# A two-layer decoder on one Trainium2 core: six of eight lanes send each token to its two experts in 128-row tiles, two lanes keep all eight experts

## Chip, core and metric

The kernel runs on one core of one Trainium2 chip. The metric is device time in microseconds (us), the median of three runs of one execution each. The engines are called as in the profile: PE (TensorE matmul), PEld (TensorE's weight load), DVE (VectorE), ACT (ScalarE), POOL (GpSimd), SP (SyncE, here only a queue that issues DMAs).

## What is computed

A decoder of two layers on x of shape (16, 128, 256), all in float32. Six blocks are added to x one after the other, each on a layer-normed x:

```python
x = x + L0_attn(ln(x))             # one causal head
x = x + L0_xattn(ln(x), ctx)       # 16 heads over a context
x = x + L0_ffn(ln(x))              # 16 blocks of 64, 4 chosen per token
x = x + L1_attn(ln(x))             # 16 heads
x = x + L1_xattn(ln(x), ctx, cell) # 16 heads, windows of 64, rotary, masked by cell
x = x + L1_ffn(ln(x))              # the experts: the block that is changed
```

The last block, with 8 experts of width 128, two of them for each token, and a shared expert of width 256 for all tokens:

```python
scores = sigmoid(x @ gate_weight.T)                    # (2048, 8)
topk_w, topk_idx = top_k(scores, 2)
topk_w = 2.5 * topk_w / (topk_w.sum(-1) + 1e-20)
h = silu(x @ w_gate[e].T) * (x @ w_up[e].T)            # for each expert e
routed = sum over the two chosen e of topk_w[e] * (h @ w_down[e].T)
out = routed + shared_swiglu(x)
```

## The kernel before

The 16 sequences are worked in 8 lanes of two sequences, 256 tokens each. A lane is a chain of Python generators: `layer_0(l)`, then `layer_1(l)` (self attention and windowed attention), then `expert_ffn(l)`. Each generator yields the engine that it wants next and the buffers it takes. The class `Turns` is a planner: it keeps an estimate of when each engine is free and when each buffer comes back, picks the thread that can go on first, and records its instructions. So the order of instructions on every engine is fixed when the program is built, by the planner's estimates; on the chip each engine works through its own list in order and waits on semaphores. All matmuls are recorded on the helper's line 126, transposes on L131, DVE work on L135, ACT on L139, POOL on L145, so the profile tells them apart by tile names.

`more()` starts lanes: at most `IN_FLIGHT = 5` at once, all eight `layer_0` first, then the eight `layer_1`, then `expert_ffn` as lanes end. The weights of the routed experts (`gu`, two tiles of 128x2048, and `down`, 128x2048) take the SBUF place of layer 0's weights, so `late_weights()` loads them after the last lane's layer 0.

`expert_ffn(l)` runs every token of a lane through all eight experts. Normalised x is transposed (`tps`), the router's scores (`rt`) are ranked, and a table of shares, zero for experts not chosen, is turned with PE (`ptt`). For each of 8 + 2 halves (8 routed experts and the shared expert's two halves) PE computes gate and up with 4 matmuls of 128x128 weights over 256 tokens (`gu`), ACT and DVE make the gated product (`sg`, `hm`), and for the routed ones PE spreads the shares over the rows (`wb`) and DVE multiplies. At the end 20 matmuls (`y1`, in the profile `y<-down,hm` and `y<-L_shared,hm`) sum all experts for both sequences, DVE adds that to x and SP stores the lane.

```python
for f in range(NE + DC):                 # one(f): 8 routed experts, 2 shared halves
    for n in range(2):                   # gate, up
        for d in range(DC):              # 256 inputs in two chunks
            q.matmul(gu[:, n, :], wt, xT[:, d, :], start=d == 0, stop=d == DC - 1)
```

A float32 matmul counts as two PE instructions in the profile, a transpose as one. Buffers are counted by `LIMITS`: 4 PSUM banks, 2 score buffers `s` (two banks each), 6 `xn`, 5 `xT`, 4 `v`, and so on. SBUF is nearly full.

Of the kernel before, what the change touches and what calls it, by code (L numbers as in the profile page):

```python
# [9 lines left out]
F32 = mybir.dt.float32  # L10
I32 = mybir.dt.int32
BF16 = mybir.dt.bfloat16
# [18 lines left out]
BPC = P // 64  # L31
NE, TOPE = 8, 2


OUT = -(2.0**100)
EPS = 1e-05
# [4 lines left out]
C_ONES = C_HEADS + HR  # L41
C_TRI16 = C_ONES + HC
C_TRI8 = C_TRI16 + NB * NB
C_ALL = C_TRI8 + NE * NE


COLS = [
# [23 lines left out]
PE, DVE, ACT, POOL, SP = "PE", "DVE", "ACT", "POOL", "SP"  # L71

WHOLE, BY_ROWS, BY_COLUMNS, BY_BOTH = range(4)


class Turns:
# [70 lines left out]
    def moved(self, n_bytes):  # L147

        self.moves = max(self.moves, self.now.at) + n_bytes / 300.0
        self.now.at = self.moves + 2000.0  # L150

    def fetch(self, out, src):

# [57 lines left out]
    def run(self, more):  # L211

        while True:
            more()
            best = None
            for i, th in enumerate(self.threads):
                if th.ask is None:
                    continue
                engine, takes = th.ask
                at = self.reach(th, engine)  # L220
                ok = True
                for tag, n in takes.items():
                    left = sorted(self.tiles[tag])
                    if not n:
                        continue
                    if len(left) < n:
                        ok = False
                        break
                    at = max(at, left[n - 1])
                if ok and (best is None or (at, th.rank, i) < best[0]):  # L230
                    best = (at, th.rank, i), th
            if best is None:
                assert not self.threads, "no thread can go on"
                return
            (at, _, _), th = best
            engine, takes = th.ask
            for tag, n in takes.items():
                self.tiles[tag].sort()
                del self.tiles[tag][:n]
            th.at, th.last = max(th.at, at), engine  # L240
            self.resume(th, None)


class Thread:
    def __init__(self, gen, rank, at, parent):
        self.gen, self.rank, self.at, self.parent = gen, rank, at, parent
        self.last, self.ask, self.waits, self.children, self.result = None, None, 0, [], None


@with_exitstack  # L250
def decoder(ctx: ExitStack, tc: tile.TileContext, a: dict, out: bass.AP):
# [4 lines left out]
    work = ctx.enter_context(tc.tile_pool(name="work", bufs=2))  # L256
    small = ctx.enter_context(tc.tile_pool(name="small", bufs=4))
    ps_s = ctx.enter_context(tc.tile_pool(name="ps_s", bufs=2, space=PSUM))
    ps = ctx.enter_context(tc.tile_pool(name="ps", bufs=4, space=PSUM))

    dram = ctx.enter_context(tc.tile_pool(name="dram", bufs=1, space=bass.MemoryType.DRAM))

    def bank(shape, name):
        return ps.tile(shape, F32, tag="bank", name=name)
# [40 lines left out]
    def along(t, n):  # L305
# [8 lines left out]

    experts = keep.tile([P, NE, P], BF16, name="experts")

    scaled_bias = {
        name: keep.tile([P, DC], F32, name=f"scaled_{name}") for name in ("L0_xattn_bq", "L1_attn_b_q", "L1_xattn_b_q")
    }
# [2 lines left out]
    for t in chosen:  # L322
        nc.gpsimd.memset(t, 0.0)

    v_tiles = [keep.tile([P, G, H * HA + CT - HA], F32, name=f"v{i}") for i in range(4)]
    for t in v_tiles:
        nc.gpsimd.memset(t, 1.0)

# [1 line left out]
    for t in tops:  # L330
        nc.gpsimd.memset(t, 0.0)


    LIMITS = dict(
        bank=4, s=2, oT=1, xn=6, xT=5, qk=5, qs=3, kb=3, v=4, p=4, oS=2, on=4, hm=8, tmp=3, rank=2, selT=2, p0=2,
        pT0=2, unseen=4, chosen=3, swap=2, words=1, top=3,
    )
    q = Turns(nc, LIMITS)

# [146 lines left out]
    def attention(qT, kb, v, j, unseen=None, to=None):  # L486
# [5 lines left out]

        js = slice(j * S, (j + 1) * S)
        yield PE, dict(s=2)
        ss = banks()
        for e in range(DC):
            for r in range(4):
# [9 lines left out]
        for t2, s in enumerate(ss):  # L507
            q.dve(
                "tensor_reduce", top[:, t2 * 2 * RT : (t2 + 1) * 2 * RT].rearrange("p (h d) -> p h d", d=HD)[:, :, 0:DC],
                s.rearrange("p r h e s -> p (r h) e s"), AX.X, ALU.max, negate=True,  # L510
            )
            q.give("s")
        yield PE, dict(bank=1)
        t = bank([P, S], "topT")
        q.transpose(t, top, ident)
# [12 lines left out]
        )  # L528
        q.give("tmp")
        yield PE, dict(s=2)  # L530
        ss = banks()
        for e in range(DC):
            for h in range(HR):
# [10 lines left out]
        def exponentials(s):  # L544
            yield ACT, dict(p=1)
            p = new("p", [P, HC, S], "p")
            q.act("activation", p, s.rearrange("p r h e s -> p (r h e) s"), AF.Exp)
            q.give("s")
            return p

        pTs = yield [exponentials(s) for s in ss]
        yield PE, dict(oT=1, bank=1)

        oT = bank([P, H // 4, S], "oT")
# [14 lines left out]
        q.act("copy", oS, oT)  # L569
        q.give("oT")  # L570
        q.give("bank")
        yield PE, dict(bank=1)
        o = bank([P, H // 4, S], "o")
        for t4 in range(H // 4):
# [327 lines left out]
        ]  # L902
        q.give("xn")

    def gated(sg, gu, h, half=0.5):

        yield DVE
        q.dve("scalar_tensor_tensor", sg, sg, 1.0, gu[:, 0, :], ALU.add, ALU.mult)
        q.dve("scalar_tensor_tensor", h, sg, half, gu[:, 1, :], ALU.mult, ALU.mult)
        q.give("tmp")  # L910
        q.give("bank")

# [51 lines left out]
    def expert_ffn(l):  # L964
# [31 lines left out]
        def one(f):  # L996
            yield PE, dict(bank=1, tmp=1)
            gu = bank([P, 2, GT], "gu")
            for n in range(2):
                for d in range(DC):  # L1000
                    if f < NE:
                        wt = w["gu"][d][:, f * D + n * P : f * D + (n + 1) * P]
                    else:
                        wt = w["shared"][:, d, n * D + (f - NE) * P : n * D + (f - NE + 1) * P]
                    q.matmul(gu[:, n, :], wt, xT[:, d, :], start=d == 0, stop=d == DC - 1)
            yield ACT
            h = hm[f // 2][:, f % 2, :]
            sg = new("tmp", [P, GT], "sg")
            q.act("activation", sg, gu[:, 0, :], AF.Tanh, scale=0.5)
            yield from gated(sg, gu, h)  # L1010
            if f < NE:
                yield PE, dict(bank=1)
                wb = bank([P, GT], "wb")
                q.matmul(wb, experts[:, f, :], wT, start=True, stop=True)
                yield DVE
                q.dve("tensor_tensor", h, wb, h, ALU.mult)
                q.give("bank")
# [15 lines left out]
            q.dve("tensor_tensor", x[l][:, j, :], x[l][:, j, :], y, ALU.add)  # L1033
            q.give("bank")
        nc.sync.dma_start(out[l * G : (l + 1) * G].rearrange("b s d -> s b d"), x[l])
        experts_ended[0] += 1


    arrives = {}
# [35 lines left out]
    def tables():  # L1075
        yield DVE
        q.dve("tensor_copy", ident16, ident)
        for name, scale in (("L0_xattn_bq", 0.25), ("L1_attn_b_q", 0.0625), ("L1_xattn_b_q", 0.25)):
            q.dve("tensor_scalar", scaled_bias[name], cols[:, slice(*COL_AT[name])], scale, None, ALU.mult)
        yield DVE  # L1080
        q.dve("memset", blocks, 0.0)
        q.dve("tensor_copy", blocks[0:NB], along(ident[0:NB, 0:NB], P // BPC))
        yield DVE
        parts = small.tile([P, NE], F32, tag="parts", name="parts", bufs=1)
        q.dve("tensor_tensor", parts, ident[:, 0:NE], ident[:, NE : 2 * NE], ALU.add)
        q.dve("tensor_tensor", parts, parts, ident[:, 2 * NE : 3 * NE], ALU.add)
        q.dve("tensor_copy", experts, along(parts, P))


    experts_ended = [0]  # L1090
    begun, ended = [0], []
    blocks_left = [NL]
    experts_begun = [0]
# [13 lines left out]
    def layer_0(l):  # L1107
        yield from causal_attention(l)
        yield from context_attention(l)
        yield from block_ffn(l)  # L1110
        blocks_left[0] -= 1
        if blocks_left[0] == 0:
            late_weights()
        ended.append(l)

    def layer_1(l):
        yield from self_attention(l)
        yield from windowed_attention(l)
        ended.append(l)

    IN_FLIGHT = 5

    def more():
        n = begun[0]
        if n < IN_FLIGHT and n not in arrives:
            return
        if n < 2 * NL and n - len(ended) < IN_FLIGHT and (n < NL or n - NL in ended[:NL]):
            begun[0] += 1
            q.start((layer_0 if n < NL else layer_1)(n % NL), n, q.free_at[PE] if n >= IN_FLIGHT else arrives[n])
            return  # L1130
        if ready and experts_begun[0] < min(len(ended) - NL, experts_ended[0] + 3):
            l = ended[NL + experts_begun[0]]
            experts_begun[0] += 1
            q.start(expert_ffn(l), 2 * NL + l, max(q.free_at[PE] - 5000, ready[0]))

    with tc.manual_schedule(engines={mybir.EngineType.PE, mybir.EngineType.DVE, mybir.EngineType.Activation, mybir.EngineType.Pool, mybir.EngineType.SP}):
        q.start(first_loads(), 0)
        q.start(tables(), 0, 16000.0)
        q.start(later_loads(), 3 * NL, 60000.0)
        q.start(hidden_by_mask(), 0, 8000.0)  # L1140
        q.start(hidden_by_window(), 3 * NL, 100000.0)
        q.run(more)

def _constants():
# [18 lines left out]
    t[:, C_HEADS : C_HEADS + HR] = np.arange(P)[:, None] // HD % HR == np.arange(HR)[None, :]  # L1165
    for n, at in ((NB, C_TRI16), (NE, C_TRI8)):
        t[:, at : at + n * n] = np.tril(np.ones((n, n)), -1).reshape(1, n * n)
    return t


# [66 lines left out]
```

## Time and profile before

| what | value |
|---|---|
| median of three runs (lowest, highest) | 850.72 us (850.51, 851.03) |
| profiled execution, its own time | 849.42 us |
| its span, first to last instruction | 847.4 us |
| PE busy | 818.3 us, 97% of the span |
| PEld, DVE, ACT, POOL busy | 661.2, 481.7, 372.1, 350.0 us |
| DMA queue of SP, share of 16 engines | 13.8% |
| TensorE clock granted, mean | 0.998 |

The page has the busy time of each engine, the span cut in 40 slices, the chain of work that ended last, and groups of instructions by tile. A group's busy time counts overlaps with the next group twice, since matmuls are pipelined; start to start distances in the timeline give the pitch at which a stream of them really runs. A "busy" PE is not waiting for another engine; whether it could do the same with fewer matmuls is not seen in that number.

### The profile page before, as it was taken

The page shows a single profiled execution, that of the slowest core. Times are in us where ns is not written, and L with a number is a line of the kernel's source. Part 1 is how long each engine was busy: PE and PEld are TensorE (multiplying, and loading weights), DVE is VectorE, ACT ScalarE, POOL GpSimd, SP SyncE. Part 2 cuts the span into 40 slices and gives each one's busy share as a digit, 9 for nine tenths or more (in the row PEclk, how much of TensorE's full clock was granted, in tenths as well). Part 3 has the DMA queues.
Part 4 walks back from the last instruction along what each step waited for, and adds up shares of the span by engine and source line. Part 5 has one row for each costly group of instructions (what it writes and reads, how often), then busy time and mean ns, then how long its engine had stood idle before and what let it go on. Part 6 is the DMA issues. An engine that isn't in the chain of part 4 may idle for free.

```text
span 847.4 us, 19890 instructions
## 1 busy us (share of the span) xinstructions
PE 818.3 (97%) x8128; PEld 661.2 (78%) x8128; DVE 481.7 (57%) x1218; ACT 372.1 (44%) x801; POOL 350.0 (41%) x606
## 2 busy tenths in 40 slices
PE   6999999999999999999979999999999999999998
PEld 5877678778787777876758867878778888888887
DVE  5446565565262644546685686675566575555533
ACT  4555434362544354626747565565343424212111
POOL 5345454153165443636777875445422331100000
PEclk9999999999999999999999999999999999999999
DMA  8325202112100000160120102010100100000000
GB/s 285 113 72 162 70 25 34 36 38 78 40 1 13 2 2 2 39 187 1 52 64 13 53 3 74 3 48 30 51 2 1 63 13 2 13 1 14 13 12 13
DMA packets 41178, 36.83 MB, mean 43 GB/s; under 512 B 6784, under 2 KB 36608, under 8 KB 40448
## 3 DMA queue, kind: packets, MB, share of 16 engines
q1 hardware_dynamic: 41088, 35.57, 13.8%
q8 instruction: 64, 1.05, 0.5%
q14 instruction: 26, 0.21, 0.1%
HBM read 27.16 MB, written 4.19 MB: 37 GB/s over the span
## 4 chain that ended last, share of the span: by engine, by line
PE 85%; DVE 6%; POOL 4%; ACT 2%; issue 2%; DMA 1%; SPq 0%; POOLq 0%; ACTq 0%; DVEq 0%
PE gu L126 16%; PE s L126 14%; PE y L126 14%; PE pj L126 11%; PE pr L126 9%; PE hp L126 7%; PE oT L126 5%; PE tps L131 3%; PE o L131 2%; PE rt L126 2%; DVE top L135 1%; POOL rstd L145 1%; DMA swap<-kT 1%; ACT p L139 1%; PE wb L126 1%
## 5 line engine op out<-in xcount | busy, mean ns | idle before, releaser
L135 DVE TENSOR_REDUCE top<-s 128x8 f32<-128x1024 f32 x96 | 112.8, 1217 | 31.1 <-PE s L126 31.0
L139 ACT ACTIVATE p<-s 128x1024 f32<-128x1024 f32 x96 | 94.6, 1027 | 60.0 <-PE s L126 60.0
L126 PE MATMUL gu<-srcT,gu 128*128 128x256 f32 x512 | 118.4, 380 | 1.5 <-DVE hm L135 0.9
L145 POOL TENSOR_TENSOR qs<-qT,less 128x512 f32<-128x512 f32 x48 | 61.0, 1272 | 112.1 <-ACT less L139 105.7
L126 PEld LDWEIGHTS gu<-srcT,gu 128*128 128x128 f32 x512 | 93.8, 190 | 16.8 <-DVE hm L135 1.2
L139 ACT ACTIVATE sg<-gu 128x256 f32<-128x256 f32 x80 | 30.8, 385 | 116.6 <-PE gu L126 111.2
L145 POOL TENSOR_SCALAR rstd<-mv 128x2 f32<-128x2 f32 x72 | 16.6, 230 | 121.0 <-DVE mv L135 116.6
L126 PE MATMUL hp<-srcT,L_w 128*128 128x256 f32 x256 | 65.9, 387 | 0.0
L126 PE MATMUL s<-qs,kb 32*128 32x128 f32 x1536 | 59.4, 286 | 5.7 <-POOL qs L145 2.9
L126 PEld LDWEIGHTS s<-qs,kb 32*128 32x128 f32 x1536 | 49.5, 188 | 16.9 <-issue 7.3
L126 PE MATMUL y<-L_w,hm 128*128 128x256 f32 x256 | 59.0, 383 | 0.0
L126 PE MATMUL y<-down,hm 128*128 128x256 f32 x256 | 58.4, 381 | 0.0
L145 POOL TENSOR_SCALAR kb<-kT,consts 128x256 f32<-128x256 f32 x96 | 53.1, 566 | 10.3 <-ACT kT L139 9.7
L126 PE MATMUL s<-kb,qT 32*128 32x256 f32 x768 | 56.5, 401 | 0.6 <-DVE top L135 0.6
L126 PE MATMUL oT<-p,v 128*32 128x128 f32 x1536 | 52.5, 276 | 2.1 <-ACT p L139 2.0
L135 DVE TENSOR_TENSOR x<-x,y 128x256 f32<-128x256 f32 x32 | 13.4, 418 | 71.4 <-PE y L126 71.4
L126 PEld LDWEIGHTS y<-L_w,hm 128*128 128x128 f32 x256 | 47.7, 190 | 8.0 <-issue 1.5
L145 POOL TENSOR_TENSOR rstd<-rstd,power 128x2 f32<-128x2 f32 x72 | 51.3, 713 | 6.0
L126 PEld LDWEIGHTS hp<-srcT,L_w 128*128 128x128 f32 x256 | 44.3, 190 | 11.5 <-issue 3.3
L126 PEld LDWEIGHTS y<-down,hm 128*128 128x128 f32 x256 | 47.8, 190 | 6.3 <-issue 0.2
L145 POOL TENSOR_TENSOR eq<-eq,consts 128x512 bf16<-128x512 bf16 (+1 forms) x16 | 15.0, 940 | 89.7 <-DVE eq L135 89.6
L135 DVE SCALAR_TENSOR_TENSOR sg<-sg,gu 128x256 f32<-128x256 f32 x80 | 33.2, 415 | 31.3 <-ACT sg L139 31.1
(149 smaller groups left out, 1625.1 us busy)
## 6 DMA issues: line engine op xcount, KB each, us to landing
unseen<-hidden SPq DMA_DIRECT2D x128, 64.0 KB, 2.4
c<-in_ctx SPq DMA_DIRECT2D x16, 256.0 KB, 3.0
x<-in_x SPq DMA_DIRECT2D x8, 256.0 KB, 6.3
L_w<-in_L_w SPq DMA_DIRECT2D x2, 1024.0 KB, 6.4
hidden<-plain SPq DMA_DIRECT2D x32, 64.0 KB, 1.5
gu<-in_L_gu SPq DMA_DIRECT2D x2, 1024.0 KB, 5.2
swap<-kT SPq DMA_DIRECT2D x16, 128.0 KB, 2.1
swap<-qT SPq DMA_DIRECT2D x16, 128.0 KB, 2.1
```

The source lines that it names most:

```text
L126: self.nc.tensor.matmul(out, lhsT, rhs, **kw)
L131: self.nc.tensor.transpose(out, src, ident)
L135: getattr(self.nc.vector, name)(out, *args, **kw)
L139: getattr(self.nc.scalar, name)(out, *args, **kw)
L145: getattr(self.nc.gpsimd, name)(out, *args, **kw)
```

## The change

Lanes 0 to 2 and lanes 3 to 5 become two groups with `GROUPS = ((0,1,2),(3,4,5))`; lanes 6 and 7 keep the eight experts for every token as before.

- `routing(l)`, at the end of `layer_1(l)` of a grouped lane: scores and ranks as before, then for each token and choice its row in a list sorted by expert (counts by five small bf16 matmuls `n`, with running totals kept in SBUF), then four indirect DMAs from POOL that scatter the normalised rows to DRAM (`to_experts`). The shared expert stays dense (`shared`).
- `plan(g)`, when a group's three lanes are routed: some 22 small DVE operations that work out for each of 19 tiles of 128 rows its expert and its rows (`tile_expert`, `tile_rows`). 19 is 2 x 768 / 128 + 7, so that each expert's last tile may be partly empty whatever the routing.
- `expert_tile(g, i)`, 19 for each group: POOL gathers 128 rows by an indirect DMA, PE transposes them (`xgt`), loads the expert's number into a PE register (`value`), and multiplies with weights whose address comes from that register: two matmuls of 256 columns for gate and up (`gu2`), a transpose (`hT2`), one for down (`y2`). ACT copies `xgT`, `hT`, `yo` and issues the DMA that stores the result in DRAM (`by_experts`).
- `combining(g, l)`, when all 19 tiles are done: four gathers by POOL for each lane, each followed by one DVE multiply-add into x; then SP stores the lane.
- `blank(g)` writes zeros over `to_experts` from SP early on.
- Lanes start in another order (`TURN`): `layer_0` of lanes 0 to 5, then `layer_1` of a lane and `layer_0` of a later one in turns. A tie in the planner goes to threads that hold the score buffers. Fewer buffers: `xn` 5 for 6, `xT` 4 for 5, `v` 3 for 4, `hm` 7 for 8, `swap` 1 for 2; 6 `xe` are new; `p0` and `pT0` 3 for 2.

```diff
+GROUPS = ((0,1,2),(3,4,5))
+    def value(self, src, most):
+        self.charge(PE, 300.0)
+        return self.nc.values_load(
+            src, engines=(mybir.EngineType.PE,), min_val=0, max_val=most,
...
+    def indexed(self, out, out_index, src, src_index):
+        at = lambda i: None if i is None else bass.IndirectOffsetOnAxis(ap=i, axis=0)
...
+        self.nc.gpsimd.indirect_dma_start(out, at(out_index), src, at(src_index))
-                if ok and (best is None or (at, th.rank, i) < best[0]):
+                key = (at, not (th.holds or "s" in takes), th.rank, i)
-        bank=4, s=2, oT=1, xn=6, xT=5, qk=5, qs=3, kb=3, v=4, p=4, oS=2, on=4, hm=8, tmp=3, rank=2, selT=2, p0=2,
-        pT0=2, unseen=4, chosen=3, swap=2, words=1, top=3,
+        bank=4, s=2, oT=1, xn=5, xT=4, qk=5, qs=3, kb=3, v=3, p=4, oS=2, on=4, xe=6, hm=7, tmp=3, rank=2, selT=2, p0=3,
+        pT0=3, unseen=4, chosen=3, swap=1, words=1, top=3,
+    def routing(l):
...
+            for j in range(G):
+                q.matmul(n[:, j, :], before, sel[:, j, :], start=True, stop=j == 0)
+                for i in range(j):
+                    q.matmul(n[:, j, :], ones, sel[:, i, :], start=False, stop=i == j - 1)
...
+            for j in range(G):
+                for k in range(TOPE):
+                    yield POOL
+                    i = j * TOPE + k
+                    q.indexed(g.to_experts, to[:, i : i + 1], xn[:, j, :], None)
...
+        yield [choice(), shared(l, xT)]
+    def expert_tile(g, i):
+        yield POOL, dict(xe=2)
+        xg = new("xe", [P, D], "xg")
+        q.indexed(xg, None, g.to_experts, g.tile_rows[:, i : i + 1])
+        yield PE, dict(bank=1)
+        t = bank([P, DC, S], "xgt")
+        for d in range(DC):
+            q.transpose(t[:, d, :], xg[:, d * P : (d + 1) * P], ident)
...
+        q.act("copy", xgT, t)
+        yield PE, dict(bank=1, tmp=1)
+        gu = bank([P, 2, P], "gu2")
+        at = q.value(g.tile_expert[0:1, i : i + 1], (NE - 1) * D)
+        for d in range(DC):
+            q.matmul(gu, xgT[:, d, :], w["gu"][d][:, bass.ds(at, D)], start=d == 0, stop=d == DC - 1)
...
+        q.act("activation", sg, gu[:, 0, :], AF.Tanh, scale=0.5)
+        q.dve("scalar_tensor_tensor", sg, sg, 1.0, gu[:, 0, :], ALU.add, ALU.mult)
+        q.dve("scalar_tensor_tensor", h, sg, 0.5, gu[:, 1, :], ALU.mult, ALU.mult)
...
+        q.transpose(t, h, ident)
+        q.act("copy", hT, t)
+        q.matmul(y, hT, w["down"][:, bass.ds(at, D)], start=True, stop=True)
+        q.act("copy", yo, y)
+        q.load(g.by_experts[i * P : (i + 1) * P, :], yo, engine=ACT)
...
+    def combining(g, l):
...
+            q.indexed(y, None, g.by_experts, by[:, j * TOPE + k : j * TOPE + k + 1])
+            q.dve("scalar_tensor_tensor", x[l][:, j, :], y, weight[l][:, j, k : k + 1], x[l][:, j, :], ALU.mult, ALU.add)
...
+    def blank(g):
...
+        for e in range(NE):
+            q.load(some, zero.to_broadcast(list(some.shape)))
+            q.now.at += 10000.0
+    def sorted_experts(g):
+        yield from plan(g)
+        yield [expert_tile(g, i) for i in range(g.tiles)]
+        yield [combining(g, l) for l in g.lanes]
+    TURN = [(0, l) for l in range(6)]
+    for l in range(NL):
+        TURN += [(1, l), (0, l + 6)] if l + 6 < NL else [(1, l)]
-        if ready and experts_begun[0] < min(len(ended) - NL, experts_ended[0] + 3):
-            l = ended[NL + experts_begun[0]]
+        dense = [l for k, l in ended if k and l not in group_of]
+        if ready and experts_begun[0] < len(dense):
+            l = dense[experts_begun[0]]
```

## The prediction

> **What bounds the kernel now.** I read the page first: busy shares, the 40 slices, the chain.
>
> ```profile
> PE 818.3 (97%) x8128; PEld 661.2 (78%) x8128; DVE 481.7 (57%) x1218; ACT 372.1 (44%) x801; POOL 350.0 (41%) x606
> ...
> PE   6999999999999999999979999999999999999998
> ...
> POOL 5345454153165443636777875445422331100000
> PE 85%; DVE 6%; POOL 4%; ACT 2%; issue 2%; DMA 1%; SPq 0%; POOLq 0%; ACTq 0%; DVEq 0%
> ```
>
> PE is busy in nearly every slice and holds 85% of the chain: work taken off PE comes off the time, unless something makes PE wait. PE idles 847.4 - 818.3 = 29.1 us. Where, the stretches say (columns: length, then PE, PEld, DVE, ACT and POOL busy, clock, DMA):
>
> ```profile
> 100.00:300.00 200.00, 199.06 (x1915) 161.00 (x1914) 104.79 (x250) 86.46 (x191) 83.68 (x135) 1.00 0.11 29
> ...
> 400.00:500.00 100.00, 93.02 (x1317) 72.22 (x1316) 71.00 (x164) 60.75 (x123) 77.71 (x132) 0.98 0.13 39
> ...
> 700.00:847.40 147.40, 143.61 (x847) 122.51 (x843) 74.04 (x217) 29.93 (x73) 9.49 (x21) 1.00 0.03 10
> ```
>
> With POOL 42% busy (83.68 of 200) PE idles 0.5 us in 100; with POOL 78% busy it idles 7.0. The last stretch is dense experts: POOL does nothing there. The price of a matmul I take from start to start in PE's timeline, since group means (380 ns for one PE instruction) hold the pipeline's tail:
>
> ```profile
> 746.15 0.27 PE L126 MATMUL wb<-selT,experts 128*128 128x256 bf16 x1
> 746.26 1.89 PE L126 MATMUL gu<-srcT,gu 128*128 128x256 f32 x8
> 747.99 0.27 PE L126 MATMUL wb<-selT,experts 128*128 128x256 bf16 x1
> ...
> 751.66 0.28 PE L126 MATMUL ptt<-ident,chosen 128*128 128x128 bf16 x2
> 751.77 0.61 PE L131 MATMUL tps<-consts,xn 128*128 128x128 f32 x4
> 752.22 3.62 PE L126 MATMUL y<-down,hm 128*128 128x256 f32 x16
> 755.67 1.03 PE L126 MATMUL y<-L_shared,hm 128*128 128x256 f32 x4
> ```
>
> Four `gu` matmuls (8 instructions) take 747.99 - 746.26 = 1.73 us, 0.4325 each; eight of `y` 3.45 us, 0.431 each; a `wb` 0.11; four transposes 0.45, 0.1125 each; two `ptt` 0.11.
>
> **PE work removed and added.** A lane that leaves the dense form loses 32 `gu` (13.84 us), 16 `y<-down` (6.90), 8 `wb` (0.88) and 2 `ptt` (0.11): 21.73 us; six lanes 130.4 us. Router, shared expert and normalisation stay. Added: five small bf16 count matmuls per lane at a `ptt`'s 0.055, 1.7 us for six. Each tile has two `gu2` (0.865), one `y2` of 256 columns (0.431) and three transposes (0.338): 1.634 us, and 38 tiles 62.1 us. The count is what is built, empty rows included: 4864 rows for 3072 choices. Net: -130.4 + 1.7 + 62.1 = **-66.6 us**.
>
> **The register load.** 38 loads of an expert's number into PE's sequencer, and 114 address computations in front of matmuls. PE's matmuls stand behind each in PE's own order, the next lane's attention too. The trace has no such load. Nearest rows below and above: PE's weight loads wait on "issue", that is on their own sequencer, and a whole fetch over a DMA queue lands after 2.4 us (first the view of waits: us in all, times, longest; then the DMA issues with KB each and us to landing).
>
> ```profile
> PEld s L126 <- issue: 12.5, 56, 0.4
> ```
>
> ```profile
> unseen<-hidden SPq DMA_DIRECT2D x128, 64.0 KB, 2.4
> ...
> hidden<-plain SPq DMA_DIRECT2D x32, 64.0 KB, 1.5
> ...
> out_x<-x SPq DMA_DIRECT2D x8, 256.0 KB, 2.1
> ```
>
> Bounds: 0 (PE has matmuls queued that run meanwhile; an added instruction gives no gain) and 38 x 2.4 = 91 us. I take 0.4 each, the longest issue wait, since a load from SBUF is nearer to an issue than to a DMA: **+15.2 us**. In the built order most loads stand one to eleven PE instructions behind a wait of the sequencer itself, so the cover is partial.
>
> [...]
>
> **POOL.** Added are 24 scatters, 38 gathers and 24 gathers for combining: 86 indirect DMAs. None is in the trace. Between POOL's smallest row (0.20 us, `less<-mv,rstd`) and the 2.4 us of a whole fetch I take the middle, 1.3 us, near POOL's 1.27 us for a 128x512 operation: 112 us. They stand in the order from about 46% of PE's work on, so in some 435 us of the span; POOL now has 350.0 - 180.1 = 169.9 us behind 400 us (180.1 is its sum in the same view up to there). That makes (169.9 + 112) / 435 = 65% busy. Between 0.5 us of PE idle per 100 us at 42% and 7.0 at 78%, 65% gives 4.7, or 20 us in 435. The present idle behind 400 us is 14.4 us, of which 3.5 is the tail counted below: 10.9. So **+8 us**, rounded down from 9. What queues behind a gather on POOL are `qs` and `rstd`, and behind these the scores on PE. This term also stands for the other order and the fewer buffers. Bounds: -10 (11.1 us of idle lie in 300 to 500, where layer 1 stands alone; mixing it with layer 0 may spread that) and +28 (2.4 us per DMA make POOL 86% busy; 9 us per 100 by extension, 39 less 10.9).
>
> In the same crowded stretch the granted clock was 0.98 over 100 us and 0.83 from 440 to 450: 1.7 us lost, and the longest PE pause in those 10 us of the timeline was 0.91. [...] The row's cost is part of the 7.0 above.
>
> **The tail.** Now it is short:
>
> ```profile
> 842.88 1.03 PE L126 MATMUL y<-L_shared,hm 128*128 128x256 f32 x4
> 843.95 0.42 DVE L135 TENSOR_TENSOR x<-x,y 128x256 f32<-128x256 f32 x1 [3.90 <-PE y L126]
> 844.40 0.37 SPq L1035 DMA_DIRECT2D out_x<-x  x1
> ```
>
> PE ends at 843.9, the span 3.5 us later. In the changed order the last `y2` is followed on PE by 2 `wb`, 8 `gu` and 20 `y` of a dense lane: 12.3 us, with the 3.5 behind it 15.8. Beside that runs a new chain: ACT copies `yo` (0.37) and issues its store (0.37), which lands (1.8, between 1.5 and 2.1), twelve gathers follow on POOL, all behind that store, the last lands (2.4), DVE adds (0.48), SP stores (0.37 + 2.1): 7.9 us and twelve gathers. At 1.3 us each 23.5 us, **+7.7** over the 15.8; at 0.2 us it is covered (0), at 2.4 us +20.9.
>
> **At nothing.** ACT gains 38 x (0.374 + 0.406 + 0.275 + 0.374 + 0.37 for the issue) = 68 us and loses 48 `sg` of 0.385, 18 us: 422 us, under PE's 752. DVE loses 48 x (0.415 + 0.421 + 0.425) = 61 us and gains about as much (76 tile operations of 0.28, 24 additions of 0.48, two plans of 22 at 0.2, some 14 more per routed lane at 0.2: 59). The 16 blanking stores of some 0.8 MB come out of SP at least 10 us apart, where the DMA engines are mostly free (0.11 busy from 100 to 300). Loads of `unseen` and `c` queue behind them; their four and five buffers let them go early. A 1 MB load lands after 5.2 us: with the cover gone, some 5 us a time; I take 0 and leave 10 for the range.
>
> **Sum.** 849.4 for the profiled execution (span 847.4 and 2.0 around it) - 66.6 + 15.2 + 8 + 7.7 = 813.7. The median of the runs shown is 1.3 above the profiled execution: **815 us**, 4.2% faster.
>
> **Rivals.**
> *The register load stalls PE (slower).* The price is P for each of 38 tiles, at `gu2`, where the sequencer fetches a value from SBUF with PE's queue drained. It decides from 815 - 15.2 + 38 P = 850.7, P = 1.34 us; at 2.4 us the time is 891. For: a wait of the sequencer shortly before most loads. Against: those waits are for results that the planned order expects earlier. 11%.
> *POOL paces the second half.* At 2.4 us per indirect DMA the POOL term is 28 and the tail 20.9: 815 - 15.7 + 48.9 = 848, nearly all given back. For: PE idles 7% where POOL is 78% busy. Against: PE waited for POOL's `qs` only 2.9 us in all. 9%.
> *The idle time evens out.* Loads covered, tail covered, order term -10: 815 - 15.2 - 7.7 - 18 = 774. For: 19 tiles fill gaps of attention. Against: fewer buffers and a busier POOL. 12%.
> That PE's work doesn't shrink can be left out: the instructions are counted in the built order; only matmuls with computed addresses could run slower than 0.43, and 0.1 us on 114 is 11 us, within the range.
>
> **Numbers.** The forecast has the remaining 68%. Its own range is 785 to 845: 15 us of loads, 8 of order and 7 of tail less, or loads at 0.8 (+15), the tail at 2 us a gather (+8) and 7 more of order. The stated range, 780 to 849, takes in POOL's rival and leaves out the slower one (11%) and half of the last (6%). About 0.2%, 1.7 us, is what a measurement of this kernel can tell from no change: faster by more 0.86, within it 0.03, slower 0.11.
>
> **What would show it.** In the changed profile: PE busy near 752 us (more means matmuls with register addresses are slow); `gu2` 76 matmuls at the pitch of `gu`; PE's idle before `gu2` under 15 us with no releaser or "issue" (over 50 us: the slower rival); POOL under 480 us and gathers start to start about 1.3 us; the span's end 20 to 25 us behind the last `y2`, with POOL, not PE, in the chain. PE idle of more than 60 us that ends at POOL's `qs` or at gathers would make the second rival right.

## The result, and the profile after

The changed kernel takes 851.88 us (median of 12 runs, 847.08 to 853.98), the kernel before on the same chip 850.62 us (12 runs): ratio 1.0007, interval [0.9991, 1.0024]. No difference, where 815 us was forecast. The profiled execution took 852.3 us, its span 850.5. From the page of the changed kernel (the rows that the prediction showed of before, and the granted clock in tenths):

```profile
PE 782.3 (92%) x7864; PEld 612.2 (72%) x7864; DVE 478.3 (56%) x1261; ACT 393.5 (46%) x899; POOL 435.1 (51%) x693
...
PE   6999999999999999999798998989998888879992
...
POOL 5343755144146348556369347684767274452304
PEclk9999999999999999999899998999999897999997
...
PE 71%; DVE 12%; POOL 6%; ACT 4%; issue 4%; DMA 1%; another core or an unknown queue 1%; ACTq 0%; POOLq 0%; DVEq 0%
```

PE is busy 36 us less, but its row is full of eights from the middle on, the clock row dips in five slices (the last of them behind PE's end), and the chain has lost 14 points of PE, most of them to DVE, POOL, ACT and issue. By stretches (length, then PE, PEld, DVE, ACT and POOL busy, clock, DMA):

```profile
100.00:300.00 200.00, 197.76 (x1927) 159.18 (x1926) 103.95 (x249) 92.14 (x203) 87.37 (x143) 1.00 0.25 78
400.00:500.00 100.00, 92.62 (x1049) 71.45 (x1048) 54.85 (x127) 50.11 (x101) 51.19 (x85) 0.95 0.16 54
600.00:700.00 100.00, 88.39 (x929) 67.72 (x914) 59.83 (x167) 52.95 (x127) 63.34 (x97) 0.96 0.21 66
700.00:850.50 150.50, 123.58 (x752) 96.23 (x750) 71.45 (x231) 47.84 (x144) 57.33 (x67) 0.91 0.27 82
```

The end, where dense lanes kept PE 97% busy (143.61 of 147.40), is now 82% busy at a clock of 0.91. Of these 150.5 us, 15.0 lie behind PE's last instruction; in the 135.6 up to it PE is 91% busy, and from 600 to 700 us, among attention and tiles, 88%. What a pause does, in the changed kernel's PE timeline (the bracket is the idle time and what ended it) and in the windows:

```profile
405.29 1.17 PE L132 MATMUL s<-qs,kb 32*128 32x128 f32 x32
...
411.99 1.12 PE L137 MATMUL tps<-consts,xn 128*128 128x128 f32 x4 [3.56 <-ACT qT L145]
413.38 2.99 PE L132 MATMUL s<-kb,qT 32*128 32x256 f32 x16 [0.28 <-ACT p L145]
```

```profile
412.00:418.80 6.80, 6.52 (x26) 4.45 (x27) 2.73 (x3) 5.95 (x12) 0.00 (x0) 0.50 0.00 0
```

PE waits 3.56 us, and then runs 6.8 us at a granted clock of 0.50. Four transposes take 1.12 us, where 0.61 was shown of before. Stretches at half clock add up to 41.0 us before PE's end, against 3.4 us in the kernel before.

The end in the changed kernel's timeline:

```profile
822.67 0.59 PE L132 MATMUL y<-down,hT 128*128 x2
...
827.92 0.94 POOL L171 DMA_INDIRECT yg<-by_experts,results  x1 [18.99 <-DVE results L141]
...
829.17 0.95 POOL L171 DMA_INDIRECT yg<-by_experts,results  x1 [0.30 <-issue]
...
834.55 1.03 PE L132 MATMUL y<-L_shared,hm 128*128 128x256 f32 x4
...
841.12 4.75 SPq L1156 DMA_DIRECT2D out_x<-x  x2
841.67 0.95 POOL L171 DMA_INDIRECT yg<-by_experts,results  x1 [0.30 <-DVE x L141]
...
844.98 0.48 DVE L141 SCALAR_TENSOR_TENSOR x<-yg,weight,x 128x256 f32<-128x256 f32 x1 [1.12 <-DMA yg<-by_experts,results]
```

Twelve gathers 1.25 us apart, the first 5 us behind the last `y2`. PE ends at 835.6, the span 15.0 us later.

So the spans differ by +3.1 us in four terms. "Work at full clock" is an estimate: PE's busy time less half of the time at half clock. It fell by 54.8 us (816.6 to 761.8). The halved clock gave back 18.8 (half of 41.0 against half of 3.4), PE's idle time before its end 27.6 (53.2 against 25.6), the tail 11.5 (15.0 against 3.5). The experiments ask where the last three come from. All of them in these terms, from their profiles (us; idle: before PE's end; tail: from PE's end to the span's). The profiled run need not be the median one: e12's took 837.80 us, e4's 845.27.

| kernel | median time | clock halved | PE work at full clock | PE idle | tail |
|---|---|---|---|---|---|
| before | 850.62 | 3.4 | 816.6 | 25.6 | 3.5 |
| changed | 851.88 | 41.0 | 761.8 | 53.2 | 15.0 |
| e1 all dense, new order | 877.34 | 17.1 | 822.0 | 41.0 | 3.8 |
| e5 all dense, TURN alone | 862.89 | 17.1 | 817.5 | 32.0 | 3.5 |
| e6 all dense, buffers alone | 875.15 | 34.1 | 818.6 | 34.1 | 3.9 |
| e10 all dense, swap alone | 864.29 | 6.8 | 820.1 | 32.9 | 3.9 |
| e18 all dense, control | 877.34 | 27.3 | 816.6 | 39.4 | 3.5 |
| e9 all dense, pauses put in | 869.93 | 13.7 | 818.0 | 39.8 | 3.5 |
| e2 fixed experts | 851.35 | 41.0 | 760.8 | 52.4 | 17.8 |
| e4 stores from SP | 842.89 | 27.3 | 763.6 | 49.3 | 16.9 |
| e7 old TURN | 847.92 | 30.7 | 763.0 | 58.2 | 11.4 |
| e8 old tie rule | 865.09 | 64.9 | 759.8 | 67.5 | 3.7 |
| e11 = e4 + e7 | 840.48 | 27.3 | 762.4 | 47.8 | 15.1 |
| e12 = e4 + swap 2 | 842.18 | 17.1 | 762.5 | 47.0 | 17.7 |
| e14 = e11 + swap 2 | 838.80 | 27.3 | 764.8 | 43.8 | 17.2 |
| e15 = e14, groups of 4 and 2 | 844.65 | 34.1 | 767.2 | 47.1 | 12.2 |
| e16 = e14 + measured prices | 834.49 | 13.7 | 764.1 | 47.6 | 13.1 |
| e17 measured prices alone | 837.28 | 20.5 | 762.6 | 46.2 | 15.0 |
| e13 no DMA by POOL | 823.36 | 23.9 | 761.9 | 43.5 | 4.2 |
| e3 one routed group | 903.81 | 47.8 | 799.0 | 74.8 | 4.0 |

### The profile page after: what moved, and what is told of

Its sections match the earlier page's. It is cut to its first block, busy times and chain, and to the rows that moved or that the text cites. A ratio compares the mean times of both kernels' runs of the same rounds, so it can differ in the third digit from the quotient of the medians.

```text
span 850.5 us, 19964 instructions
## 1 busy us (share of the span) xinstructions
PE 782.3 (92%) x7864; PEld 612.2 (72%) x7864; DVE 478.3 (56%) x1261; ACT 393.5 (46%) x899; POOL 435.1 (51%) x693
## 4 chain that ended last, share of the span: by engine, by line
PE 71%; DVE 12%; POOL 6%; ACT 4%; issue 4%; DMA 1%; another core or an unknown queue 1%; ACTq 0%; POOLq 0%; DVEq 0%
PE s L132 14%; PE y L132 9%; PE pj L132 9%; PE pr L132 9%; PE gu L132 8%; PE hp L132 8%; PE oT L132 5%; DVE top L141 2%; PE tps L137 2%; PE o L137 2%; POOL rstd L151 2%; PE rt L132 2%; ACT p L145 1%; DMA yg<-by_experts,results 1%; PE ot L137 1%
## 5 line engine op out<-in xcount | busy, mean ns | idle before, releaser
L132 PE MATMUL s<-kb,qT 32*128 32x256 f32 x768 | 60.2, 412 | 2.6 <-ACT p L145 2.0
L171 POOL DMA_INDIRECT xg<-to_experts,tile_rows x38 | 37.6, 990 | 45.5 <-PE xgt L137 19.1
L141 DVE SCALAR_TENSOR_TENSOR sg<-sg,gu 128x128 f32<-128x128 f32 (+1 forms) x70 | 24.1, 344 | 58.5 <-ACT sg L145 53.5
L132 PEld LDWEIGHTS hp<-srcT,L_w 128*128 128x128 f32 x256 | 45.6, 195 | 11.4 <-issue 2.2
L145 ACT ACTIVATE sg<-gu 128x128 f32<-128x128 f32 (+1 forms) x70 | 22.8, 326 | 65.6 <-PE gu L132 50.1
L145 ACT ACTIVATE hm<-hp,cols 128x256 f32<-128x256 f32 x64 | 26.8, 470 | 54.5 <-PE hp L132 53.9
L132 PEld LDWEIGHTS s<-kb,qT 32*128 32x128 f32 x768 | 37.5, 189 | 18.2 <-issue 7.1
L132 PEld LDWEIGHTS oT<-p,v 128*32 128x32 f32 x1536 | 39.6, 111 | 14.6 <-issue 5.7
L145 ACT COPY oS<-oT 128x512 f32<-128x512 f32 x48 | 28.2, 588 | 45.2 <-PE oT L132 45.1
L137 PE MATMUL tps<-consts,xn 128*128 128x128 f32 x224 | 36.5, 285 | 11.8 <-DVE xn L141 7.0
```

The lines of the kernel that those rows point to most:

```text
L132: self.nc.tensor.matmul(out, lhsT, rhs, **kw)
L137: self.nc.tensor.transpose(out, src, ident)
L141: getattr(self.nc.vector, name)(out, *args, **kw)
L145: getattr(self.nc.scalar, name)(out, *args, **kw)
L171: self.nc.gpsimd.indirect_dma_start(out, at(out_index), src, at(src_index))
```

## The experiments

### e1, e2, e3, e4: order, register loads, half the routing, ACT's stores

**e1**, all lanes dense in the new order:

```diff
-GROUPS = ((0,1,2),(3,4,5))
+GROUPS = ()
-    ... xe=6, hm=7, ...
+    ... xe=6, hm=8, ...
```

> All eight lanes dense, in the changed kernel's order of lanes, with its rule for ties and its smaller buffers (hm 8 for 7, which five dense lanes need). Theory A (the saved PE work is given back by PE's pauses around the routed tiles, by the halved clock behind those pauses, and by the tail): the order itself costs little, 846 to 856 us, PE idle 25 to 32 us, clock 0.99 or more. Rival B (the order and the smaller buffers cost the time): 870 to 890 us, with PE idle 45 us or more and a clock near 0.97 without any routed tile.

877.34 us, ratio 1.0321 [1.0303, 1.0338]. Rival B in time: without one routed tile the changed kernel's order is 26.6 us slower than before. Between the profiles of e1 and of the changed kernel, which share the rules of the order and all buffers but one `hm`, the span falls by 24.8 us: 60.2 us of PE work go, 12.0 come back by the clock, 12.2 by idle time, 11.2 by the tail. So the routing brings something, and the step from before to e1 takes it. The two share the rules, not the order: PE's recorded instructions part at 45 us.

**e2**, the expert of each tile fixed when the program is built:

```diff
-        at = q.value(g.tile_expert[0:1, i : i + 1], (NE - 1) * D)
+        at = min(i * NE // g.tiles, NE - 1) * D
-            q.matmul(gu, xgT[:, d, :], w["gu"][d][:, bass.ds(at, D)], ...)
+            q.matmul(gu, xgT[:, d, :], w["gu"][d][:, at : at + D], ...)
...
-        q.matmul(y, hT, w["down"][:, bass.ds(at, D)], start=True, stop=True)
+        q.matmul(y, hT, w["down"][:, at : at + D], start=True, stop=True)
```

> The changed kernel with each tile's expert fixed when the program is built (a constant for each tile, so the choice of weights is left out of the computation): no register load, no computed address, all matmuls, DMAs and their order otherwise alike. Theory A: the loads are covered, 847 to 853 us. Rival C (register loads and computed addresses hold PE): at the 0.4 us a load of the prediction 836 us, at 1 us or more a load under 815 us.

851.35 us against 851.88: Theory A in time. But the order is not alike, as the expectation had it: the planner charges 0.3 us for a load, and without that charge PE's order differs from 585 us on, with two of the 38 tiles' `gu2` before that point. So the equal times alone don't prove it. The changed kernel's waits of PE are the firmer evidence (us, times, longest; all its rows for `gu`, dense and tiles):

```profile
PE gu L132 <- DVE hm L141: 4.7, 2, 4.2
...
PE gu L132 <- ACT xgT L145: 1.2, 3, 0.8
...
PE gu L132 <- issue: 0.4, 1, 0.4
PE gu L132 <- ACT yo L145: 0.4, 1, 0.4
...
PE gu L132 <- ACT hT L145: 0.2, 1, 0.2
```

Of 6.9 us, 0.4 has no releaser but issue, which means that the profile shows nothing waited for, and that wait stands before a dense `gu` (at 788.26 us). Directly before the 228 instructions with computed addresses PE idles 4.5 us in all, 0.05 of it at issue. So 38 register loads and 114 computed addresses cost at most 4.5 us.

**e3**, one group:

```diff
-GROUPS = ((0,1,2),(3,4,5))
+GROUPS = ((0,1,2),)
```

> Lanes 0 to 2 in one routed group, lanes 3 to 7 dense. PE's work is 33 us less than before by the prediction's prices (3 x 21.73 - 0.85 - 19 x 1.634). Theory A: the group is done long before the end and dense lanes stand behind it, so there is no tail and fewer pauses: 822 to 836 us, clock 0.985 or more, PE idle under 40 us. Rival B (order and buffers) has no gain: 850 us or more. If what is given back goes by the number of routed tiles, half of the changed kernel's result: 849 to 853 us.

903.81 us, ratio 1.0626: Theory A missed, and rival B's "850 us or more" holds, though none foresaw a loss of 53 us. No tail, as expected (4.0), but the most idle time of all kernels. Its tiles run from 617.6 to 724.7 us; much of the loss lies before any of them:

```profile
300.00:400.00 100.00, 85.91 (x794) 67.06 (x793) 44.49 (x128) 40.35 (x87) 50.38 (x84) 0.93 0.10 30
400.00:500.00 100.00, 89.24 (x1022) 66.51 (x1021) 53.94 (x133) 45.44 (x91) 51.12 (x88) 0.90 0.14 48
```

No tile is at work there. The first scatter comes at 385.7 us; from 300 to 385 us, with neither tile nor scatter, PE idles 14.1 us at a clock of 0.92, and that loss is the recorded order's. From 700 to 800 us, with the last tiles, PE idles another 16.5.

**e4**, results stored by SP:

```diff
-        q.load(g.by_experts[i * P : (i + 1) * P, :], yo, engine=ACT)
+        yield SP
+        q.load(g.by_experts[i * P : (i + 1) * P, :], yo)
```

> The changed kernel with the 38 stores of tile results issued by SP in place of ACT. Theory A: ACT's issues are a small part of the pauses, 846 to 854 us. Rival D (ACT, held by 38 issues of 0.33 us and by what they wait for, is late with its copies): 12 us or more faster, 840 us or less, with the ACT-ended idle of PE down by as much.

842.89 us, ratio 0.9905 [0.9889, 0.9922]: between the two expectations. By its terms the gain is 6.9 us by the clock (13.7 us less at half) and 3.9 us less idle. But PE's first 6798 instructions are the changed kernel's in the same order (ACT's order differs from the first store on, at 580 us), and there e4 gains nothing: the next one starts at 659.6 us, in the changed kernel at 656.2, with seven of the 38 stores issued in each. All of the gain lies behind that point, where PE's recorded order differs, so it is not shown that ACT's stores cost it; PE's idle that ends at ACT fell by 4 us (27.4 to 23.4), not by the 12 or more of rival D.

### e5, e6, e7, e8, e10: which part of the order

**e5**: before, with TURN alone. **e6**: before, with the buffers alone. **e10**: before, with `swap` 1 alone.

```diff
# e5
-        if n < 2 * NL and n - len(ended) < IN_FLIGHT and (n < NL or n - NL in ended[:NL]):
+        if n < 2 * NL and n - len(ended) < IN_FLIGHT and (TURN[n][0] == 0 or (0, TURN[n][1]) in ended):
...
# e6
...
-        bank=4, s=2, oT=1, xn=6, xT=5, ..., v=4, ..., hm=8, ..., p0=2, pT0=2, ..., swap=2,
+        bank=4, s=2, oT=1, xn=5, xT=4, ..., v=3, ..., hm=7, ..., p0=3, pT0=3, ..., swap=1,
# e10
-        ... swap=2,
+        ... swap=1,
```

> The kernel before with one thing changed: lanes start in the changed kernel's order (TURN). All lanes dense, buffers and tie rule of before. Theory B1 (of the 26.6 us that all-dense lost in the changed order, buffers and ties, TURN is the cause): 868 to 880 us, with a PE pause of several us near 280 to 290 us and 10 us of halved clock behind it. Rival B2 (the smaller buffers or the tie rule are the cause): 847 to 855 us.

> The kernel before with one thing changed: the changed kernel's numbers of buffers (xn 5, xT 4, v 3, hm 7, swap 1, p0 and pT0 3). All lanes dense, order of lanes and tie rule of before. Theory B1 (TURN is the cause): 848 to 855 us. Rival B2 (buffers are the cause): 865 to 880 us, PE idle over 35 us.

> The kernel before with one buffer changed: swap 1 for 2, so that only one rotation of q or k in the windowed attention is under way. All lanes dense. If swap is what the smaller buffers cost: 862 to 875 us. If the cost lies in xn, xT, v or hm: 847 to 855 us.

862.89 (ratio 1.0132), 875.15 (1.0256, [1.021, 1.0303]) and 864.29 us (1.0154). e6 and e10 fall where the buffers, or `swap`, are the cause, e5 between its two theories. Each edit alone costs 12 to 24 us; e6 already holds the `swap` of e10, and TURN and buffers together, in e1 (with the new tie rule and `hm` 8), cost 27, not 12 + 24: no sum. This looked like several causes until the control below.

**e7**: changed, with the old order of lanes. **e8**: changed, with the old tie rule.

```diff
# e7
-    TURN = [(0, l) for l in range(6)]
-    ...
+    TURN = [(k, l) for k in range(2) for l in range(NL)]
# e8
-                key = (at, not (th.holds or "s" in takes), th.rank, i)
+                key = (at, th.rank, i)
```

> The changed kernel with one thing undone: lanes start as before, all eight of layer 0 and then layer 1; six lanes routed, buffers and tie rule as changed. Theory B1: what the order took comes back, 822 to 838 us. Rival B2: no more than 5 us from the changed kernel, 847 to 857 us. Rival E (the old order leaves both groups' tiles and gathers to the end, and the tail grows): 855 us or more, with over 25 us from the last y2 to the span's end.

> The changed kernel with one thing undone: a tie in the planner goes by rank again and not to the holder of the score buffers. Theory B1: 846 to 858 us, the tie rule matters little. Rival B3 (the tie rule is what makes the pauses): 835 us or less.

847.92 us (0.9957) and 865.09 us (1.0168). The old TURN gives 4 us back (rival B2) where Theory B1 expected 14 to 30. The old tie rule costs 13 us, outside both expectations: with it PE has 64.9 us of halved clock. Whether that is the rule's work or that of one more order, a single recorded order can't tell. In e8 the last gather starts at 845.5 us, 14 ahead of PE's end, so the tail is only 3.7 us; the idle time of 67.5 outweighs it.

### e18 and e9: the control, and what a pause costs

**e18**, before with one planning price a tenth higher:

```diff
-    SWITCH = 91.0
+    SWITCH = 100.0
```

> A control: the kernel before, with one price of the planner changed by a tenth (91 to 100 ns for PE's change of shape). Buffers, order of lanes and work are those of before; the recorded order differs in most places. Theory I (the smaller buffers themselves cost the 24 us of e6): 848 to 858 us. Rival H (the order of before is simply a lucky one, and any other order costs as much): 865 to 880 us.

877.34 us, ratio 1.0321 [1.0303, 1.034]: rival H, and as slow as e1. Work, buffers and lanes are those of before; only the recorded order differs. PE's work at full clock is the same 816.6 us; the span is longer by 13.8 us of idle time and 12.0 of halved clock. From its page, and a pause in its PE timeline:

```profile
PE   6999999999999898999898899999999999999998
...
PEclk9999999999999998999799999999999999999999
```

```profile
422.03 1.15 PE L126 MATMUL s<-kb,qT 32*128 32x256 f32 x16
423.11 1.13 PE L126 MATMUL pr<-L_o,oT 128*128 128x256 f32 x4
427.03 3.21 PE L126 MATMUL s<-kb,qT 32*128 32x256 f32 x16 [2.79 <-DVE top L135]
```

The same sixteen score instructions take 1.15 us before a pause of 2.79 us and 3.21 behind it. Five all-dense kernels in other orders (e1, e5, e6, e10, e18) lie 12 to 27 us above before, none near it. So before's order is one of few waits, and all five edits that recorded a new one gave it up; the 24 us of e6 can't be put down to the buffers. Only e18 changes nothing but the order; it is one control.

**e9**, pauses put in ahead of the dense `gu`, order kept:

```diff
+    POWERS = {5: 1, 6: 2, 7: 5}
...
+    def pause(gu, n):
...
+        q.transpose(gu[:, 0, 0:P], ident, ident)
...
+        q.act("activation", held, gu[:, 0, 0:G], AF.Exp)
+        for _ in range(n):
+            q.pool("tensor_tensor", held, held, power, ALU.pow)
+        q.transpose(gu[0:G, 1, 0:P], held, ident)
...
             gu = bank([P, 2, GT], "gu")
+            if f in (2, 6):
+                pause(gu, POWERS.get(order, 0))
```

> The kernel before, its order kept instruction for instruction, with six pauses of PE put in ahead of gu matmuls of the last three dense lanes, where PE is 99% busy: PE transposes, ACT reads the result, POOL does one (two pauses), two (two pauses) or five (two pauses) powers of about 0.75 us, PE waits for that. The pauses should be about 1.3, 2.0 and 4.4 us long, some 15.5 us in all, read from the profile. Theory F (a pause of somewhat over 1 to 2 us already halves the granted clock for 3.4 us or more behind it, and the pause is so paid a second time): 15.5 us and 1.7 to 3.4 us for each of the four longer pauses, 873 to 881 us, with 14 us or more of halved clock from 700 us on. [...]

869.93 us, 18.9 above before. PE's pauses in its timeline and the clock in its windows:

```profile
798.62 0.27 PE L131 MATMUL gu<-consts,held 128*2 128x128 f32 x1 [1.87 <-POOL held L145]
...
808.21 0.27 PE L131 MATMUL gu<-consts,held 128*2 128x128 f32 x1 [1.85 <-POOL held L145]
...
832.35 0.37 PE L131 MATMUL gu<-consts,held 128*2 128x128 f32 x1 [4.16 <-POOL held L145]
832.52 3.62 PE L126 MATMUL gu<-srcT,gu 128*128 128x256 f32 x8
...
846.77 0.27 PE L131 MATMUL gu<-consts,held 128*2 128x128 f32 x1 [4.16 <-POOL held L145]
```

```profile
795.00:810.00 15.00, 11.28 (x57) 9.09 (x56) 6.90 (x17) 2.27 (x8) 2.76 (x4) 1.00 0.03 8
...
830.70:837.50 6.80, 5.15 (x14) 3.93 (x15) 1.07 (x3) 0.38 (x1) 1.44 (x3) 0.50 0.00 0
```

Theory F missed: less than its 873 to 881 us, with 10.2 us of halved clock behind the pauses and not 14. The pauses were 1.32, 1.09, 1.87, 1.85 and twice 4.16 us, 14.5 in all. Behind the first four the clock stays 1.00; the long ones are followed by 6.8 and 3.4 us at 0.50, where eight `gu` instructions take 3.62 us and not 1.89. By half of those 10.2 us, the six pauses cost 14.5 + 5.1 = 19.6 us, about what was measured.

No pause between 1.87 and 4.16 us was tried in e9. Elsewhere halved clock followed shorter ones than 4.16: in e18 a pause of 2.79 us was followed by 13.7 us at half clock (clock 0.60 from 424 to 441 us), and in the changed kernel one of 1.77 us, with 0.41 shortly before, by 6.8 (0.69 from 514 to 525 us). Dense `gu` stand around the pauses of e9, attention, transposes or the router around the others; what decides was not tried.

### e11, e12, e14, e15: do the gains add up

**e11** is e4 with the TURN of e7. **e12** is e4 with `swap` 2 and `hm` 6. **e14** has all three. **e15** is e14 with other groups:

```diff
-GROUPS = ((0,1,2),(3,4,5))
+GROUPS = ((0,1,2,3),(4,5))
```

> Six lanes routed, with two changes to the changed kernel: stores of tile results from SP, and lanes start as before (all of layer 0 first). Apart they brought 9 and 4 us. If they act on different waits: 836 to 842 us. If every change of the recorded order deals out the pauses anew: anything between 835 and 860 us, and no sum of the two.

> Six lanes routed, stores of tile results from SP, swap back to 2 buffers and hm 6 for 7 to make the room. If swap is the buffer that costs: 825 to 835 us (15 us or half of the buffers' 24). If not: 838 to 848 us.

> Six lanes routed with three changes to the changed kernel: stores of tile results from SP, lanes started as before, swap 2 with hm 6. The full-speed work of PE (busy time less half of the halved clock) should stand at 762 us as in all kernels with six routed lanes. If the three act on different waits: 832 to 838 us. If each new order deals out the pauses anew: 835 to 850 us, idle 45 to 58 us.

> As e14, with groups of four and two lanes in place of three and three: 38 tiles again (23 and 15), but eight gathers at the end for twelve. Four gathers less at 1.25 us should take 5 us off the tail; 15 tiles in place of 19 at the end should leave fewer of them without attention beside them. If the tail and the last group's tiles are a price of their own: 826 to 834 us, with 10 to 13 us from PE's end to the span's end. If not: e14's time within 4 us, or more.

840.48, 842.18, 838.80 and 844.65 us. The sum of e4 and e7 fits e11 (838.9 expected from 9 and 4), but `swap` adds nothing to e4, and e14 is within 2 us of e11, so not the sum of three. e15 has its five us less of tail (12.2 for 17.2) and loses 9.1 again: 3.3 of idle, 3.4 by the clock (6.8 us more at half) and 2.4 of work.

### e13: POOL's DMAs taken away

```diff
     def indexed(self, out, out_index, src, src_index):
-        self.charge(POOL, 1100.0 if out_index is not None else 1600.0)
+        self.charge(SP, 350.0)
...
-        self.nc.gpsimd.indirect_dma_start(out, at(out_index), src, at(src_index))
+        if out_index is None:
+            self.nc.sync.dma_start(out, src[0:n, :])
+        else:
+            self.nc.sync.dma_start(out[self.rows : self.rows + n, :], src)
...
```

The first branch is a gather, the second a scatter; the choice of rows is left out.

> The changed kernel with its 86 indirect DMAs by POOL replaced by plain DMAs of fixed rows from SP (the choice of rows is left out of the computation). POOL is back at its 350 us of before; PE's work, the tiles' chains and the bytes moved are the same. If POOL's share (the indirect DMAs standing ahead of rstd, qs and kb) makes the pauses and the tail: PE idle before its end under 38 us for 53, a tail under 10 us for 15, 825 to 838 us. If the chains of the tiles themselves and the lack of dense work between them make the pauses: idle 46 us or more, 842 to 856 us.

823.36 us, ratio 0.9675 [0.9656, 0.9693]. Against the changed kernel the span is 29.0 us shorter: 10.8 of tail, 9.7 of idle, 8.6 by the clock, nothing of PE's work. From its page:

```profile
PE 773.9 (94%) x7864; PEld 609.2 (74%) x7864; DVE 468.2 (57%) x1261; ACT 393.9 (48%) x899; POOL 352.2 (43%) x607
...
PE   6999999999999999999999999999999888989967
```

PE's row is whole up to the 31st slice; about half of the idle time that is left (20.6 of 43.5) lies behind 636 us, among tiles and dense lanes. Of the two theories the first is right on the tail, 1.6 us under its range in time, and half right on idle (under 38 expected, 46 or more by the other). The tail's part goes with the twelve gathers; the rest may hold the luck of one more order, which parts from the changed kernel's at 381 us.

### e16, e17: measured prices for the planner

```diff
-        self.charge(POOL, 1100.0 if out_index is not None else 1600.0)
+        self.charge(POOL, 1250.0)
-        self.charge(PE, 300.0)        # value
+        self.charge(PE, 0.0)
```

> As e14, with the planner's prices set to what the profile shows: 1.25 us of POOL for a gather or a scatter (was 1.6 and 1.1), none of PE for a register load (was 0.3). If the pauses come from a planned order that rests on wrong prices: 8 us or more below e14. If they come from the chains themselves: within 6 us of e14.

> The changed kernel with only the planner's prices set to the measured ones (1.25 us of POOL for a gather or a scatter, none of PE for a register load). In the kernel with the three other edits this brought 4 us. If the right prices help by themselves: 840 to 849 us. If the gain there was the luck of one order: anywhere between 845 and 865 us.

**e16**, with e14's edits, 834.49 us, ratio 0.9811 [0.9794, 0.9827]: 4.3 below e14. **e17**, on the changed kernel alone, 837.28 us, ratio 0.9849: 14.6 below it, more than expected. The new prices helped both times, but by 4 and by 15 us, and a price moved without need cost 27 (e18): so the gain can't be put down to the prices being right. For the scatter the old 1.1 was the nearer one: it holds POOL for 1.05 us. e16 beats both kernels, with the least halved clock of all routed ones (13.7 us).

## Why the prediction was wrong

**The base of the sum and the order term (+8).** This is the step that failed. The sum starts from before's 849.4 us and lets +8, with 28 as the upper bound, stand for POOL's share, "the other order and the fewer buffers" and, within POOL's rows, the clock behind short waits. Measured between the two profiles it is 46.4 us: 27.6 of idle before PE's end and 18.8 by the halved clock. Of the 38.6 us by which the profiled execution lies above the 813.7 of the sum, this term is 38.4; the errors of the others (work 11.8 too hopeful, loads 15.2 too dear, tail 3.8 too small) cancelled but for 0.4, by luck.

The mechanism was wrong too: the term was read off POOL's share, as if PE's waits followed it. e18 has POOL's 606 instructions and 349.1 us busy, as before (350.0), and 13.8 us more idle with 12.0 more by the clock. So the recorded order alone moves this term by 25.8 us, and before's order, the base, had few waits: five all-dense kernels in other orders took 862.9 to 877.3 us, +12 to +27. How the 46.4 us divide between the order and POOL's DMAs stays open; e13, without these DMAs, has 18.3 less of the two, but in a new order again. "The idle time evens out" at -10 did not come: TURN alone gave 6.4 us more idle (e5), the whole new order 15.4 (e1).

An estimate over the recorded orders: ten kernels with six routed lanes (without e2 and e13, which leave out a choice) took 834.5 to 865.1 us, median 842.5; the six all-dense ones without pauses put in, 850.6 to 877.3, median 869.7. By that the routing is worth some 27 us, where 36 were forecast; the orders are few and not drawn at random.

**PE's work (-66.6).** Too large by 11.8. PE is busy 782.3 us and not 752. 20.5 of the 30.6 us between are halved clock; at full clock it is 761.8, a gain of 54.8. The price of a matmul holds in a stream: in the changed kernel's timeline four `gu2` instructions take 790.96 - 790.09 = 0.87 us, as counted.

```profile
790.09 1.03 PE L132 MATMUL gu<-gu,xgT 128*128 x4
790.96 0.59 PE L132 MATMUL y<-down,hT 128*128 x2
```

Nine of the other ten us are the tiles' own. From each tile instruction to PE's next, or to its own end where PE then idles, and with half of the halved clock taken off, the trace has 71.2 us for 38 tiles, 1.87 each, where 62.1 and 1.63 were counted. The median instruction of `gu2` and `y2` takes 0.216 us, as counted, the mean 0.23 and 0.24, and a tile's transposes 0.15 and 0.16 for 0.11: in these short pieces PE did not keep the pitch of the stream. e1 has 5.4 us more than before at the same work, so an order can move this number too.

**The clock.** Seen in one row (0.83 for 10 us) and counted inside another term; it cost 18.8 us, more than the tail. e18, with 27.3 us at half clock, shows that it needs no routed tile; another order is enough.

**The register load (+15.2).** At most 4.5 us, and nothing in time (e2). Its lower bound was right. The slower rival, P of 1.34 us or more, is out. Dropping this term would have made the forecast 800, further off.

**POOL and the tail (+8, +7.7).** The gather's price was right (1.25 us apart, 1.3 taken), and POOL's 435.1 us are under 480. What went wrong is what follows: the span ends 27.2 us behind the last `y2` (850.5 - 823.3), not 20 to 25, and PE's work behind that `y2` covers 12.3 of it as counted, so the tail is 15.0 us and +11.5 over before's, where +7.7 stood. e13 puts 28.5 us on POOL's DMAs in all, order's luck included, where the sum had 15.7 for both. The second rival named this and the time (848), but not by its price: a DMA takes 1.25 us and not 2.4, POOL is 51% busy, and PE's idle (53.2, under the 60 asked for) ends at ACT and DVE, behind POOL only at second hand. At 408 us ACT waits 5.46 us for POOL's additions to x, and PE for ACT's `qT`.

**At nothing.** DVE flat (478.3 against 481.7) holds; ACT came to 393.5, not 422; whether its stores were free is open, since e4 is 9 us faster only where its order differs.

Put together with the measured terms: 849.4 - 54.8 (work) + 0 (loads) + 46.4 (waits before PE's end, and the clock) + 11.5 (tail) = 852.5, where 852.3 was profiled. The sum shows sizes; the causes behind the third are only in part told apart.

## What to carry to other kernels

When a program builds its order from planned times, the kernel before holds one order out of many, and its time is that order's. Before an edit is priced against it, record the same work in another order (a price changed by a tenth does it): if that costs 27 us, an edit that should bring 66 has to pay this first, and experiments that move the time by less than that can't tell a cause by themselves. Where an experiment records a new order, compare the traces up to the point where the orders part: e4 had gained nothing there. And PE's pauses want a term for the clock behind them: the halved clock took 18.8 us more in the changed kernel than before, and 12.0 more in e18.

## What the runs showed of the hardware

- A pause of PE of 4.16 us was followed by 3.4 or 6.8 us at half clock, pauses of 1.1 to 1.9 us between dense matmuls by none (e9); a 2.79 us one among attention by 13.7 us (e18). In the kernel before, 3.4 us at half clock (in 440 to 450 us) came with no pause over 0.91 us in these ten.
- Loading a register of PE from SBUF, and addresses computed from it in front of matmuls, cost at most 4.5 us over 38 loads (PE's idle directly before these matmuls in the changed kernel); a kernel without them took 851.35 against 851.88 us.
- An indirect DMA of 128 rows of 1 KB holds POOL 0.95 (a gather of results) to 1.05 us (a scatter). Gathers came every 1.25 us in a row; a scatter straight behind another came 2.8 to 2.9 us after it, and POOL waited 1.7 us (changed kernel, three times).
